# A Mamba-2 block with LoRA experts: the gates of six groups moved out of the scan into a stage of their own

## The chip, the cores and the metric

The kernel runs on one core of a Trainium2 chip, in one launch. The metric is the device time in microseconds (us). Engines: TensorE (PE in the profile; PEld is its weight load), VectorE (DVE), ScalarE (ACT), GpSimd (POOL) and SyncE (SP), whose queue issues all DMAs here. All data are fp32; a matmul of this kernel shows as two records of TensorE.

## What is computed

The input is x, 2048 tokens of 1024 channels. It is normalised (layer norm), goes through a Mamba-2 layer and a LoRA mixture, and both are added to x. The parts that matter here:

```python
proj = einsum('bld,pd->blp', xn, in_proj_w)      # gate 4096 | hbc 6144 | dt 64
gate, hbc, dt = proj[..., :4096], proj[..., 4096:10240], proj[..., -64:]
xBC = silu(causal_conv4(hbc))                    # x: 64 heads of 64; B, C: 8 groups of 128
state = state * dA_t + dtx_t * B_t               # the scan, over 2048 steps
y = state @ C_t + x * D
yn = y * rsqrt(mean(y * y over a group of 512) + eps) * norm_weight
yn = yn * silu(gate)
out = yn @ out_proj_w.T
result = x + out + (xn @ W_base.T + b_base) + lora
```

Each of the eight groups has 512 of the 4096 gate channels: four tiles of 128.

## The kernel before

**Tiling.** Channels lie on partitions, in tiles of 128. The tokens are cut into two halves of 1024 (s = 0, 1), each half into two of 512, each of these into four chunks of 128. A block is one (half, group, 512 tokens): 32 blocks of four chunks, 128 chunks.

**Products of one level.** Each input projection is done in pairs of output tiles, [2 tiles x 1024 channels] by [1024 channels x 1024 tokens], as a 2 x 2 block product with seven products in place of eight (Strassen's scheme in Winograd's form). `pair` (L450) makes the seven products, each of four matmuls with 512 columns, and adds them up in PSUM and in two temporary tiles. Their right operands, seven sums of blocks of xn, stay in SBUF for a half (`ops_of`); the left ones are weight blocks and four sums of them, made by GpSimd in `left_operands` (L413; the sums are L427) in the first half, stored, and loaded again in the second. Seven products leave four quarters. Per pair, ScalarE copies one product (L474), VectorE makes two temporaries (L478, L482) and three of the quarters (L531), ScalarE the fourth quarter (L529). `stored` (L523) then writes each quarter to DRAM; for a gate it passes through a SiLU on ScalarE first: L533, on what VectorE wrote in L531.

**The stream of pairs.** `in_pairs` (L557) yields the pairs: for each half and group, three for x, B and C and two for the gate; at last eight for the base weights, the second half before the first. 88 pairs, 616 products. `products(n, side)` takes n products from the stream and interleaves small steps of other work (side).

**The scan.** The main loop (L978) runs the chunks. One chunk: a product; the norm's mean if a block begins; `scan_b` (L731: the products ps_y, ps_e, ps_st with the chunk's operands, then ecp, y and the state on VectorE, the state's decay on GpSimd); the decay scan es of the next chunk on VectorE (L688, from dab, which a DMA brings); a product; `scan_a`'s ps_cb and its masked product with es (L702, dab); further products; transposes ps_xt, from which ScalarE makes xdt (L713) and xdd (L721). The convolution of the next block (L646 on VectorE, with SiLU L653 on ScalarE), the norm's squares (L797, L802) and the norm with the gate (L819, L822, L830) run as side steps; `norm_gate` multiplies by the gate (loaded by `load_gate`) and stores y. `plan` (L968) sets how many products have been taken by each chunk: 35 before the first, 315 after 60 chunks, 602 after 128. So a chunk takes four or five. From block 15 on, `out_sums` (L864) makes the block sums of the output weights on GpSimd (L83, tiles wo), one sixteenth per block; blocks 2 to 13 of the first half also carry the layer norm of the second half's tokens, in pieces that begin at blocks 2, 5, 8 and 11.

**The output stage.** Behind the scan the last 14 products of the stream run, then the output projection: four passes (half, half of the channels), each a product of [8 tiles x 2048 channels] by [2048 channels x 1024 tokens] in two levels: seven units of seven products, a product being eight matmuls with 256 columns. Order of the passes: second half of the tokens first.

**The order of the work.** Matmuls and transposes (`mm`, `transpose`) keep their program order; so do the SiLU of the convolution, xdt and xdd. Other instructions may be moved by the scheduler that builds the program.

```python
def products(n, side):
    ...
    for i in range(n):
        next(stream)
...
            products(1, parts[0])
            ...
            scan_b(*blk, c)
            ...
            products(1, parts[1])
            next(a, None)
            products(1, parts[2])
            products(1, parts[3])
            next(a, None)
```

Of the kernel before, what the change touches and what calls it, by code (L numbers as in the profile page):

```python
# [13 lines left out]
L = 2048  # L14
# [20 lines left out]
KH = KT // 2  # L35
NW = 12
PRE = 5
POST = 2
# [4 lines left out]
def mamba_lora_kernel(  # L43
# [19 lines left out]
    dram = ctx.enter_context(tc.tile_pool(name="dram", bufs=1, space=bass.MemoryType.DRAM))  # L63
    const = ctx.enter_context(tc.tile_pool(name="const", bufs=1))
    in_ctx = ExitStack()
    op = in_ctx.enter_context(tc.tile_pool(name="op", bufs=1, side="right"))
    wp = in_ctx.enter_context(tc.tile_pool(name="wp", bufs=NW, side="right"))
# [489 lines left out]
    def in_pairs():  # L557
        for s in range(NS):
            ops = lambda s=s: ops_of["x", s]
            for g in range(G):  # L560
                if s and g == 0:
                    load_ops(s)
                for q, (i0, i1) in enumerate(((0, 1), (2, 3), (4, 5))):
                    tis = [4 * g + i if i < 4 else 32 + 8 * (i - 4) + g for i in (i0, i1)]
                    key, name = f"x{g}_{q}", f"x_{s}_{g}_{q}"
                    quarters = halves(*(w_in[32 + t] for t in tis))
                    to = stored(raw_d[g], i0, s, AF.Copy)
                    if s + g + q:
                        yield pair(key, name, quarters, ops, to, s == 0)
                    else:  # L570
                        yield plain_pair(key, name, quarters, to)
                for q in range(2):
                    t = 4 * g + 2 * q
                    yield pair(
                        f"g{g}_{q}", f"g_{s}_{g}_{q}", halves(w_in[t], w_in[t + 1]), ops,
                        stored(gate_d[g], 2 * q, s, AF.Silu), s == 0,
                    )
# [8 lines left out]

    N_IN = NS * (5 * G + 4)
    stream = ahead(in_pairs())
# [195 lines left out]

    def load_gate(s, g, half):
        sg = p1.tile([P, 4, TB], F32, tag="sg", name=f"sg_{s}_{g}_{half}")
        at = s * TS + half * TB
# [28 lines left out]
    def norm_gate(s, g, half):  # L816
# [11 lines left out]
        for j in (0, 2):  # L828
            two = xg[:, j : j + 2, :]
            nc.vector.tensor_tensor(two, two, sg_of[s, g, half][:, j : j + 2, :], ALU.mult)  # L830
            nc.sync.dma_start(y_d[g][:, j : j + 2, at : at + TB], two)
            yield
# [17 lines left out]
    def base_sums(pool, i):  # L850
# [7 lines left out]
        for j, what in ((3, "s1"), (4, "s2"), (5, "s3"), (6, "s4")):  # L858
            d = dram.tile([P, KH, P], F32, tag=f"{what}_b{i}", name=f"{what}_b{i}_d")
            nc.sync.dma_start(d, t[:, j])  # L860
            kept[f"b{i}", what] = d
        yield

# [103 lines left out]

    plan = [(0, 7 * PRE), (n_slots // 2 - NQ, 7 * (5 * G + 5)), (n_slots, total)]  # L968

# [8 lines left out]
    for b, blk in enumerate(blocks):  # L978
# [16 lines left out]
        for c in range(NQ):  # L995
# [28 lines left out]
            a = scan_a(*follow) if follow else iter(())  # L1024
            parts = [side[i * len(side) // n : (i + 1) * len(side) // n] for i in range(n)]

# [3 lines left out]
            scan_b(*blk, c)  # L1030
            if b == 14 and c:
                next(left_sums)
# [15 lines left out]
            products(1, parts[2])  # L1048
            products(1, parts[3])
            next(a, None)  # L1050
# [4 lines left out]
            if b == 14:  # L1055
                left_sums = base_sums(wo, c)
                next(left_sums)
            if 0 <= b - 15 < 16 and c == 0:
# [13 lines left out]
            if (after, c) in ((1, 1), (2, 0)):  # L1072
                next(rest)
    norm_mean(*blocks[-1])
    for _ in norm_gate(*blocks[-1]):
# [6 lines left out]

    oa = ctx.enter_context(tc.tile_pool(name="oa", bufs=1, reuse_waits="tile"))
    ow = ctx.enter_context(tc.tile_pool(name="ow", bufs=7, reuse_waits="tile"))
    ot = ctx.enter_context(tc.tile_pool(name="ot", bufs=5, reuse_waits="tile"))
    passes = [(s, p) for s in (1, 0) for p in range(2)]
    units = (1, 2, 5, 7, 6, 3, 4)
    inner = (1, 6, 5, 2, 7, 3, 4)
    HT = TB // 2

# [21 lines left out]
    quarter_of = {}  # L1112
    place_pool = [oa] * 2

    def load_quarter(t, k, n):
# [6 lines left out]
        for h in range(2):  # L1122
            x = place_pool[place].tile(
                [P, KH, TB], F32, tag=f"q{place}_{h}", name=f"q_{t}_{k}{n}_{h}"
            )
            nc.sync.dma_start(x, y_d[4 * p + 2 * k + h][:, :, at : at + TB])
            parts.append(x)
# [36 lines left out]

    load_hw(1)
    for _ in range(7 * POST - 5):
        next(stream)
    next_ops = {}
    for _ in level_two(quarter_of[0, 0, 0], "0_0", next_ops):
        pass  # L1170
    for _ in stream:
        pass
    in_ctx.close()
    ob = ctx.enter_context(tc.tile_pool(name="ob", bufs=1, side="right", reuse_waits="tile"))
# [55 lines left out]
    load_quarter(0, 0, 1)  # L1230
    load_acc(1, 0, 0)

    kept_sum = None
    for t, (s, p) in enumerate(passes):
        last = t + 1 == len(passes)
        for u, i in enumerate(units):
# [16 lines left out]
            if t == 0 and u < 2:  # L1253
                if u == 0:
                    at(3, load_quarter, 0, 1, 1)
                    at(5, load_acc, 1, 0, 1)
                else:
                    at(1, load_acc, 1, 1, 1)
                    at(4, load_acc, 1, 1, 0)
            for u0, n, quarter in ((2, 0, (0, 0)), (4, 2, (1, 0)), (6, 1, (0, 1)), (6, 2, (1, 1))):  # L1260
# [10 lines left out]
            if p == 1:  # L1271
# [3 lines left out]
                if not last:  # L1275
                    for u0, n, quarter in ((2, 4, (0, 0)), (6, 3, (1, 1)), (6, 5, (0, 1))):
                        if u == u0:
                            at(n, load_acc, s - 1, *quarter)
            elif t and u == 0:
# [123 lines left out]
```

## Time and profile before

| | |
|---|---|
| median of 3 runs | 3451.87 us (3450.51 to 3454.31) |
| the profiled execution | 3453.59 us; its span 3451.8 us |
| TensorE | 3409.2 us busy, clock granted 0.997 |
| VectorE | 2501.2 us busy |
| ScalarE | 1164.7 us busy |
| GpSimd | 696.1 us busy |
| DMA | 769.83 MB, mean 223 GB/s |
| first ps_y of the scan, last ps_y | at 184.4 us, at 2678.5 us |

How to read it: the times of single instructions come from the profiled execution. A group of instructions is named by line, engine, operation and the tiles written and read; behind it stand its count, the busy time and the mean length, and what ended the idle time before it. A table by stretches gives each engine's busy time in a piece of the span. In the waits a line reads: who waited, for whom, us in total, times, longest. A busy TensorE is one that has a matmul in it.

### The profile page before, as it was taken

What the parts mean: (1) busy time and instruction counts of PE and PEld (TensorE: products, weight loads), DVE (VectorE), ACT (ScalarE), POOL (GpSimd) and SP (SyncE); (2) the same over time, 40 slices, a digit from 0 to 9 for tenths busy, and PEclk for the clock granted to TensorE, in tenths of its full rate; (3) what the DMA queues carried; (4) which work ended last, traced back from release to release, by engine and by line L of the source; (5) the groups of instructions that cost most, each with busy time, mean ns of one, the idle gap of its engine ahead of it and who ended that gap; (6) DMA issues with size and microseconds to landing.
All of it is one profiled execution on the core that took longest, in us unless ns stands there. A gap on an engine that the chain in (4) does not pass through costs nothing.

```text
span 3451.8 us, 38274 instructions
## 1 busy us (share of the span) xinstructions
PE 3409.2 (99%) x12818; PEld 1992.3 (58%) x12818; DVE 2501.2 (72%) x2861; ACT 1164.7 (34%) x3182; POOL 696.1 (20%) x443
## 2 busy tenths in 40 slices
PE   9999999999999999999999999999999999999999
PEld 7444544544545544454455445444444588888888
DVE  7548877877977877777787877777775466566665
ACT  2234453444444443444445444444442100000000
POOL 3122223222222211322223232222321000000000
PEclk9999999999999999999999999999999999999999
DMA  6546655655666676887778887777778687586654
GB/s 235 186 166 197 205 191 186 211 187 197 203 200 204 205 254 219 291 256 231 236 242 260 236 258 244 245 237 236 228 239 267 243 277 242 196 299 188 214 164 146
DMA packets 530324, 769.83 MB, mean 223 GB/s; under 512 B 35152, under 2 KB 264656, under 8 KB 527440
## 3 DMA queue, kind: packets, MB, share of 16 engines
q1 hardware_dynamic: 530128, 767.39, 68.7%
q8 instruction: 102, 1.67, 0.2%
q14 instruction: 94, 0.77, 0.1%
HBM read 516.64 MB, written 250.61 MB: 222 GB/s over the span
## 4 chain that ended last, share of the span: by engine, by line
PE 84%; DVE 9%; issue 3%; ACT 2%; DMA 1%; POOL 0%; SPq 0%; DVEq 0%; ACTq 0%; POOLq 0%
PE ps_x_x L79 12%; PE ps_x_w L79 8%; PE ps_a_x L79 8%; PE ps_y_x L79 8%; PE ps_x_g L79 7%; PE ps_a_w L79 6%; PE ps_y_w L79 6%; PE ps_y_g L79 5%; PE ps_a_g L79 4%; PE ps_y L79 3%; PE ps_e L79 3%; PE ps_st L79 2%; PE ps_x_b L79 2%; DVE xg L646 2%; PE ps_a_b L79 2%
## 5 line engine op out<-in xcount | busy, mean ns | idle before, releaser
L83 POOL TENSOR_TENSOR state<-state,tot 128x512 f32<-128x512 f32 x112 | 153.7, 1373 | 1326.0 <-PE ps_e L79 1199.8
L688 DVE TENSOR_TENSOR_SCAN es<-dab,here 128x1024 f32<-128x1024 f32 x128 | 304.6, 2380 | 83.4 <-ACT xdd L721 81.8
L646 DVE SCALAR_TENSOR_TENSOR xg<-rawx,cw,xg 128x512 f32<-128x512 f32 x384 | 339.2, 933 | 18.7 <-ACT xg L640 18.0
L79 PE MATMUL ps_x_w<-t,w 128*128 128x256 f32 x1344 | 303.8, 379 | 0.0
L713 ACT ACTIVATE xdt<-ps_xt,dt 128x64 f32<-128x64 f32 x1024 | 223.8, 333 | 209.7 <-PE ps_xt L88 209.7
L79 PEld LDWEIGHTS ps_x_w<-t,w 128*128 128x128 f32 x1344 | 255.4, 190 | 41.5 <-issue 7.7
L721 ACT ACTIVATE xdd<-xdt,es 128x64 f32<-128x64 f32 x1024 | 261.9, 388 | 0.0
L1340 ACT COPY s<-ps_a_w 128x512 f32<-128x512 f32 x28 | 16.4, 586 | 636.0 <-PE ps_a_w L79 555.5
L83 POOL TENSOR_TENSOR wo<-wo 128x512 f32<-128x512 f32 (+1 forms) x112 | 213.4, 1906 | 6.8
L79 PE MATMUL ps_a_w<-q,w 128*128 128x256 f32 x896 | 202.5, 379 | 0.0
L702 DVE TENSOR_TENSOR dab<-es,cbm 128x1024 f32<-128x1024 f32 x128 | 180.1, 1407 | 29.6 <-ACT cbm L698 29.6
L79 PEld LDWEIGHTS ps_a_w<-q,w 128*128 128x128 f32 x896 | 170.2, 190 | 23.6 <-issue 0.5
L79 PEld LDWEIGHTS ps_y<-dab,xdt 128*64 128x64 f32 x2048 | 114.6, 139 | 105.1 <-ACT xdd L721 38.7
L79 PE MATMUL ps_x_x<-op_again,s_x 128*128 128x512 f32 x384 | 172.7, 592 | 0.0
L79 PE MATMUL ps_y_x<-op_again,s_x 128*128 128x512 f32 x384 | 172.7, 592 | 0.0
L79 PE MATMUL ps_a_x<-op_again,a_x 128*128 128x512 f32 x384 | 172.7, 592 | 0.0
L79 PE MATMUL ps_x_x<-op,s_x 128*128 128x512 f32 x368 | 165.5, 592 | 0.0
L79 PE MATMUL ps_y_x<-op,s_x 128*128 128x512 f32 x368 | 165.5, 592 | 0.0
L79 PE MATMUL ps_a_x<-op,a_x 128*128 128x512 f32 x368 | 165.4, 592 | 0.0
L79 PE MATMUL ps_y<-dab,xdt 128*64 128x128 f32 x2048 | 146.6, 284 | 7.8 <-ACT xdt L713 7.8
L531 DVE TENSOR_TENSOR ev<-ps_x_x,s_x 128x512 f32<-128x512 f32 x94 | 64.5, 687 | 120.5 <-PE ps_x_x L79 116.1
L646 DVE SCALAR_TENSOR_TENSOR bc<-rawb,cw,bc 128x512 f32<-128x512 f32 x192 | 145.7, 790 | 1.9 <-ACT bc L640 1.0
(236 smaller groups left out, 6118.6 us busy)
## 6 DMA issues: line engine op xcount, KB each, us to landing
w<-w SPq DMA_DIRECT2D x196, 512.0 KB, 3.7
dab<-da_d SPq DMA_DIRECT2D x128, 512.0 KB, 5.5
raw<-ev SPq DMA_DIRECT2D x192, 256.0 KB, 3.3
a_x<-in_w_in_dram SPq DMA_DIRECT2D x168, 256.0 KB, 4.2
w<-wo SPq DMA_DIRECT2D x96, 448.0 KB, 4.3
ecp<-run_d SPq DMA_DIRECT2D x256, 128.0 KB, 4.0
gate<-ev SPq DMA_DIRECT2D x128, 256.0 KB, 3.9
sg<-gate SPq DMA_DIRECT2D x32, 1024.0 KB, 7.8
```

Source lines behind the costliest of these rows:

```text
L79: tc.keep_in_program_order(nc.tensor.matmul(*args, **kw))
L83: ins = nc.gpsimd.tensor_tensor(*args)
L531: nc.vector.tensor_tensor(e, ps, add, alu)
L646: nc.vector.scalar_tensor_tensor(dst[:, i, :], raw[:, i, k : k + TB], cw[:, ti, k : k + 1], dst[:, i, :], ALU.mult, ALU.add,)
L688: nc.vector.tensor_tensor_scan(es.rearrange("p h t -> p (h t)"), dab.rearrange("p h t -> p (h t)"), here, 0.0, ALU.mult, ALU.add,)
L702: nc.vector.tensor_tensor(ms, es, cbm.unsqueeze(1).to_broadcast([P, HG, Q]), ALU.mult)
L713: ins = nc.scalar.activation(xdt[:, h, :], x_t[:, h, :], AF.Copy, scale=dt_of[s][:, half * NQ + c, at : at + 1],)
L721: ins = nc.scalar.activation(xdd[:, h, :], xdt[:, h, :], AF.Copy, scale=es[:, h, Q - 1 : Q])
L1340: nc.scalar.copy(s1, pa)
```

## The change

Six of the eight groups (g < 6; an oct is two groups, eight tiles, and there are `NO = 3` octs) no longer have gate pairs in the stream. It has 64 pairs, 448 products; the plan's marks are 35, 224 after 60 chunks, 434 after 128, so a chunk takes three or four, and a fourth is only taken when the plan asks for it. In these groups `norm_gate` stores the norm without a gate, and no gate is loaded there.

Behind the stream a new stage makes the gates: for each half and each oct a product of [8 tiles x 1024 channels] by [1024 channels x 1024 tokens] in two levels: seven units (outer products) of seven inner products, each inner product four matmuls with 256 columns. The outer left sums are made on GpSimd (`oct_sums`): the first oct's in the last block of the scan, the others' in the new stage; `left_two` makes the inner ones on GpSimd for each unit. The inner right sums are made on VectorE (`right_two`) and kept for the half's three octs; the seven outer right sums of the second half are loaded again (`load_again`). Finished quarters are passed through a SiLU, multiplied by the stored norm, which is loaded for it, and stored to yg_d (`gated`). The output stage reads yg_d for these groups and takes the first half of the tokens first.

```diff
+NO = 3
...
-                for q in range(2):
+                for q in range(2 if g >= 2 * NO else 0):
...
-    N_IN = NS * (5 * G + 4)
+    N_S = 5 * G - 4 * NO
+    N_IN = NS * (N_S + 4)
...
     def load_gate(s, g, half):
+        if g < 2 * NO:
+            return
...
-            nc.vector.tensor_tensor(two, two, sg_of[s, g, half][:, j : j + 2, :], ALU.mult)
+            if g >= 2 * NO:
+                nc.vector.tensor_tensor(two, two, sg_of[s, g, half][:, j : j + 2, :], ALU.mult)
             nc.sync.dma_start(y_d[g][:, j : j + 2, at : at + TB], two)
...
+    def oct_sums(pool, tag, o, i):
...
+        for j, src in enumerate(halves(w_in[at], w_in[at + 2])):
+            nc.sync.dma_start(t[:, j], src)
+        yield
+        a11, a12, a21, a22 = (t[:, j] for j in range(4))
+        add(a22, a21, a22, ALU.add)
+        add(a21, a11, a21, ALU.subtract)
+        add(a11, a22, a11, ALU.subtract)
+        add(a12, a12, a11, ALU.subtract)
+        for j, src in ((5, a22), (7, a21), (6, a11), (3, a12)):
+            nc.sync.dma_start(s_d[o][j][:, q, m], src)
...
-    plan = [(0, 7 * PRE), (n_slots // 2 - NQ, 7 * (5 * G + 5)), (n_slots, total)]
+    plan = [(0, 7 * PRE), (n_slots // 2 - NQ, 7 * (N_S + 4)), (n_slots, total)]
...
-            products(1, parts[3])
+            products(min(n - 3, 1), parts[3])
...
+    order = (1, 2, 6, 5, 7, 3, 4)
+    gate_units = [(s, o, i) for s in range(NS) for o in range(NO) for i in order]
...
+    def left_two(u):
...
+        add(s1, a21, a22, ALU.add)
+        yield
+        add(s2, s1, a11, ALU.subtract)
+        yield
+        add(s4, a12, s2, ALU.subtract)
+        yield
+        add(a21, a11, a21, ALU.subtract)
+        yield
...
+    def gated(s, o, a, n, z):
...
+        for q in range(2):
+            nc.sync.dma_start(y[:, q], y_d[2 * o + q][:, 2 * a : 2 * a + 2, at])
+        yield
+        for q in range(2):
+            nc.scalar.activation(z[:, q], z[:, q], AF.Silu)
+            yield
+        for q in range(2):
+            nc.vector.tensor_tensor(z[:, q], z[:, q], y[:, q], ALU.mult)
+            nc.sync.dma_start(yg_d[2 * o + q][:, 2 * a : 2 * a + 2, at], z[:, q])
+            yield
...
+        if i == 2:
+            nxt[0].append(lambda a=c11, b=k_: big_add(a, b))
...
+        def put(m, n, ps, add):
+            dst = out[:, :, m, n * HT : (n + 1) * HT]
+            if i in (1, 2, 5, 7):
+                if add is None:
+                    nc.scalar.copy(dst, ps)
+                else:
+                    nc.vector.tensor_tensor(dst, ps, add, ALU.add)
+            else:
+                for part in (ps, add):
+                    if part is not None:
+                        nc.vector.tensor_tensor(dst, dst, part, ALU.add)
+
+        left, right = left_of.pop(u), right_of[s, i]
+        for n, j in enumerate(inner):
+            ps = {1: pa, 2: pa, 6: px, 7: px, 4: px, 5: py, 3: py}[j]
+            for q in range(2):
+                for k in range(KQ):
+                    mm(
+                        ps[:, q, :], left[j][:, q, k, :], right[j][:, k, :],
+                        start=(n < 3 and q + k == 0), stop=(k == KQ - 1), skip_group_check=True,
+                    )
...
+            for step in side[n]:
+                step()
...
-    passes = [(s, p) for s in (1, 0) for p in range(2)]
+    passes = [(s, p) for s in range(NS) for p in range(2)]
...
-            nc.sync.dma_start(x, y_d[4 * p + 2 * k + h][:, :, at : at + TB])
+            g = 4 * p + 2 * k + h
+            nc.sync.dma_start(x, (yg_d if g < 2 * NO else y_d)[g][:, :, at : at + TB])
```

## The prediction

> **What bounds the kernel now.** I read four views: the page, a table by stretches, the waits, and the timeline of a spot where TensorE stands still. The page first:
>
> ```profile
> span 3451.8 us, 38274 instructions
> ...
> PE 3409.2 (99%) x12818; PEld 1992.3 (58%) x12818; DVE 2501.2 (72%) x2861; ACT 1164.7 (34%) x3182; POOL 696.1 (20%) x443
> ...
> PE   9999999999999999999999999999999999999999
> PEld 7444544544545544454455445444444588888888
> DVE  7548877877977877777787877777775466566665
> ```
>
> TensorE is busy everywhere, and it has two stages: a scan stage (slices 3 to 31; VectorE at 7 to 8 tenths) and an output stage (VectorE at 6). The table by stretches puts numbers on both (columns: stretch, length, then busy time of PE, PEld, DVE, ACT, POOL, clock, DMA share, GB/s):
>
> ```profile
> 400.00:1400.00 1000.00, 988.23 (x3528) 504.54 (x3527) 779.30 (x994) 453.75 (x1213) 235.67 (x155) 1.00 0.64 208
> 1400.00:2600.00 1200.00, 1183.31 (x4291) 594.17 (x4290) 935.78 (x1003) 522.36 (x1482) 338.27 (x191) 1.00 0.78 244
> ```
> ```profile
> 1094.50:1182.70 88.20, 88.20 (x327) 47.25 (x326) 75.03 (x98) 38.92 (x106) 21.82 (x15) 1.00 0.63 206
> 2551.00:2625.30 74.30, 74.30 (x273) 37.34 (x272) 58.92 (x59) 30.56 (x90) 21.31 (x12) 1.00 0.74 237
> 3000.00:3200.00 200.00, 200.00 (x912) 173.05 (x911) 126.11 (x137) 5.27 (x9) 0.00 (x0) 1.00 0.72 240
> ```
>
> VectorE has 78% in the scan stage and TensorE loses only 11.8 + 16.7 = 28.5 us of 2200. The single stretches are one block (four chunks) each: block 11, which also carries a layer norm, block 30, and the output stage. Block 11 has VectorE at 85% and no idle TensorE, so a full VectorE alone doesn't stop it. Where TensorE does stand still, the waits and a timeline (VectorE, then ScalarE) tell why:
>
> ```profile
> ACT ev L533 <- DVE ev L531: 175.7, 63, 7.6
> ```
> ```profile
> 2304.70 5.43 DVE L797 SCALAR_TENSOR_TENSOR xg<-xg,dsk,y 128x512 f32<-128x512 f32 x4
> ...
> 2317.49 0.68 DVE L531 TENSOR_TENSOR ev<-ps_y_g,s_g 128x512 f32<-128x512 f32 x1
> ```
> ```profile
> 2318.20 0.63 ACT L533 ACTIVATE ev<-ev 128x512 f32<-128x512 f32 x1 [3.22 <-DVE ev L531]
> 2318.74 1.73 ACT L713 ACTIVATE xdt<-ps_xt,dt 128x64 f32<-128x64 f32 x8
> ```
>
> VectorE runs late (four L797 take 5.43 us where the median of one is 0.745 us), so the SiLU of a gate's eviction waits 3.22 us at the head of ScalarE's queue, and xdt (L713), on which TensorE's next scan products wait, stands behind it. TensorE loses 2.6 us there. Only gate pairs have that SiLU.
>
> **The change part by part.** *Removed from the scan:* 2 halves x 6 groups x 2 = 24 gate pairs of 7 products of 4 matmuls. One product takes 3.43 us (timeline of TensorE: one starts at 1899.68, what follows it at 1903.11): 168 x 3.43 = 576 us of TensorE. *Added behind it:* 2 x 3 x 7 = 42 units of 28 matmuls with 256 columns. The output stage runs just this shape: 912 records in 200 us, two a matmul, 0.2193 us a record, 56 records a unit: 12.28 us, 516 us in all. TensorE's own work falls by 60 us: seven eighths of the products are left, each at 2% more per column.
>
> *VectorE in the scan.* A gate pair's five adds (L478, L482, L531: 0.68 us) go, 0.49 us a product; so do two gate multiplies (L830, 1.217 us) in three blocks of four. Products per block fall from 18.7 to 12.6 in the first half (189 in 60 chunks by the new plan) and from 16.9 to 12.35 in the second (210 in 68). Block 30 (17 products): TensorE 74.3 - 4.65 x 3.43 = 58.3; VectorE 58.9 - 2.3 - 2.4 = 54.2 us, 93%. Block 11 (19): TensorE 88.2 - 22.0 = 66.2; VectorE 75.0 - 3.1 - 2.4 = 69.5: VectorE is over. GpSimd's sums for fresh weights (L427, 1.4 to 2.1 us, four a pair) fall by 0.9 pair in a first-half block, some 5 us less to collide with, worth 0 to 5 us of VectorE; I take 2. Over the four layer-norm blocks (85 to 87% now) the excess is 8 to 18 us; I take 12.
>
> *A rule against it.* The Trainium skill (Perfetto Trace Analysis, Optimization Strategy) says that where the most-contended engine changes from stage to stage, interleaving the stages may help. This change takes interleaving away: TensorE work that filled a VectorE-heavy stage gets a stage of its own. By the rule all that VectorE can't follow is lost; by the rows VectorE's total stays below TensorE's but in the layer-norm blocks, so the 12 us are all that throughput costs. The rest is a question of waits.
>
> *Waits in the scan* (28.5 us now). Some 15 us end behind the gate's SiLU; with a quarter of these pairs left, -11. The other 17 come of evictions and xdt that reach VectorE late. Its spare share goes from 22% to 7%, and waits for a queue grow about as the inverse: 17 to 52, +35. From both sides: +0 if they stay (blocks 8 and 11 have none at 85%), +88 if they grow sixfold. I take 35, since the trace's fullest blocks lie nearer to none.
>
> *Chunks lose one product of cover.* es starts as soon as xdd (L721) is done, its product with cbm (L702) is done 4 us or more before TensorE needs it; one product less leaves about 1 us: counted in the 35.
>
> *The new stage.* Per unit VectorE has five or nine adds of 0.69 us, with the gating and operand sums 51 us (68 in a half's first oct) of an oct's 86: covered. A product here is 1.75 us, and one accumulator (product 7, then 4) must be read within that: one add of 0.69 us fits, a 1.22 us multiply ahead of it doesn't. 0 to 1 us a unit; nearest row, the output stage, loses nothing with 3.5 us: 0.15 x 42 = 6 us. ScalarE's SiLU: 8 of 1.06 us an oct, covered. GpSimd: 4 sums a unit (L427 1.4 us, 5.6) and 4 more in 8 units: 11.2 of 12.28 us, covered, barely. DMA: weights 7 MB, gate in and out 8 MB, block sums 8 MB: 23 MB in 86 us, 267 GB/s; the page has slices of 299 with TensorE full. SP issues some 50 more in an oct, 0.4 us each, behind no wait but a store's, with units loaded two ahead. In the scan SP loses gate stores and loads. The last oct's gating lies beside output products; the new order of the halves costs nothing, since the last gates are read only in the fourth pass; the hand-over between stages waits for tiles freed five units earlier: 0 to 5 us, taken at 0 for that reason. The sums of the first oct in the last block use GpSimd at 1.6 us of 17 busy: 0.
>
> *The sum.* -60 - 11 + 35 + 12 + 6 = -18 us. The profiled execution took 3453.6 us (span 3451.8), the median of the runs is 3451.9; from that median 3434 us.
>
> **The rivals.** *No new waits:* blocks 8 and 11 as the model for all; waits keep their 17 us: 3451.9 - 60 - 11 + 12 = 3393; without the layer-norm excess 3381. For it: zero idle at 85%. Against: VectorE's spare falls to a third.
>
> *VectorE falls behind GpSimd (slower).* The output weights' sums take 20 us of GpSimd in each block of the second half, the weight sums much the same in the first. The skill (SBUF — State Buffer, Who interferes with whom) calls the shared port an exclusive lock: an operation with two SBUF inputs blocks while GpSimd reads. The four L797 lost 2.45 us to 4.5 us of such sums, about half, not all; by the rule a block would lose up to 20 us, by that row about 10, and the 54.2 us have this in them already. But the chunks that follow had 9 us of idle VectorE to catch up in; now it is about 1 us a chunk, so the lag of chunk 3 lasts into the convolution of chunk 1. Price: 3.5 us in each of 30 blocks, 105 in place of the 52: 3487. It decides from 60 + 11 - 12 - 6 = 53 us of added waits, 1.8 us a block.
>
> *Half of that* (2 us a block): 3451.9 within 0.2%, no change.
>
> *The short evictions:* 1 us lost in each unit and in each oct's catching up: +45, 3479. Against: VectorE is at 60 to 79% there.
>
> *It doesn't do what it says:* the diff drops 672 matmuls of 512 columns and issues 1176 of 256; no reading of it leaves the counts as they were. Excluded.
>
> **How the numbers follow.** Likeliest 3434 (0.45, own range 3410 to 3444); no new waits 3390 (0.12); half the lag 3452 (0.12); full lag 3487 (0.24); short evictions 3479 (0.07). A measurement tells about 0.2%, 7 us, from no change: faster 0.57, same 0.12, slower 0.31. The range 3388 to 3492 leaves out about 1 in 10 on either side.
>
> **What would show it.** Right: blocks of the second half of 59 to 61 us with 12 or 13 products, VectorE at 90 to 93%, the L533 wait down to a quarter, 42 units of 12.3 to 12.5 us. Wrong: blocks over 62 us with TensorE waiting on xdt or L531 (lag), ScalarE held by L802 or L653 in the SiLU's place, units over 13 us (evictions, GpSimd), or a gap before the output stage.

## The result, and the profile after

The changed kernel takes 3549.13 us (median of 4 runs, 3547.47 to 3550.23), beside 3453.09 us for the kernel before on the same chip: ratio 1.0278, 95% interval 1.0261 to 1.0296. It is slower by 96 us; the forecast was 18 us faster, and the time lies outside the range.

The page of the kernel after, its first lines and the rows of TensorE and VectorE:

```profile
span 3546.5 us, 40663 instructions
...
PE 3386.6 (95%) x13826; PEld 2202.4 (62%) x13826; DVE 2733.4 (77%) x3103; ACT 1187.5 (33%) x3179; POOL 973.4 (27%) x611
...
PE   9999998998999899999989999999999999999999
...
DVE  7568888888889798889889888666766676666665
```

TensorE was 9 in every slice before; now there are slices of 8, all of them in the scan, where VectorE has 8 and 9. The span grew by 94.7 us, so the time is lost inside the program. The table by stretches places it. First the kernel before (first half of the scan, second half, output stage), then the kernel after (the same, with the new stage as third line). The first number behind a stretch is its length, the second TensorE's busy time, the fourth VectorE's; the granted clock is third from the end:

```profile
184.40:1496.50 1312.10, 1299.98 (x4635) 659.95 (x4634) 1005.59 (x1237) 582.73 (x1589) 329.53 (x214) 1.00 0.64 209
1496.50:2678.50 1182.00, 1165.66 (x4238) 585.83 (x4239) 903.92 (x966) 507.12 (x1462) 313.59 (x176) 1.00 0.78 243
...
2742.40:3451.80 709.40, 704.48 (x3201) 607.81 (x3199) 446.40 (x472) 18.75 (x32) 0.00 (x0) 1.00 0.65 218
```
```profile
184.10:1252.90 1068.80, 996.02 (x3875) 526.85 (x3874) 906.47 (x1140) 549.88 (x1526) 257.84 (x166) 0.97 0.63 203
1252.90:2236.70 983.80, 932.59 (x3664) 481.48 (x3663) 865.60 (x894) 479.79 (x1413) 351.20 (x183) 0.99 0.82 252
...
2297.10:2833.90 536.80, 515.84 (x2354) 447.39 (x2352) 347.16 (x382) 86.53 (x115) 284.47 (x192) 0.99 0.64 218
2833.90:3546.50 712.60, 706.63 (x3200) 608.85 (x3200) 453.25 (x478) 19.20 (x33) 0.00 (x0) 1.00 0.67 227
```

Length less busy time is TensorE's idle time. In the scan it rises from 12.1 + 16.3 = 28.4 us to 72.8 + 51.2 = 124.0 us; the new stage adds 21.0, the output stage 1.1. Over the whole span it goes from 42.6 to 159.9 us: **+117**. TensorE's busy time in the scan should have fallen by the 576 us of the removed products, from 2465.6 to 1889.6; it is 1928.6, **39 us more than its work**. The new stage is busy for 515.84 us, the 516 of the forecast. So the span's +95 is -60 (less work) + 117 (idle) + 37 to 39 (the same work at a lower clock; 37 over the whole span: 3409.2 - 60 = 3349 would have been TensorE's busy time, it is 3386.6).

**Whom TensorE waits for.** The waits of TensorE, before and then after:

```profile
PE ps_nv L79 <- ACT xdt L713: 10.5, 4, 3.3
PE ps_y L79 <- ACT xdt L713: 7.8, 5, 4.6
```
```profile
PE ps_y L81 <- ACT xdt L716: 40.1, 11, 9.6
PE ps_xt L90 <- ACT bt L703: 34.4, 19, 7.5
PE ps_var L81 <- DVE lsq L266: 9.2, 3, 6.1
```

Both large ones name ScalarE, which is busy for a third of the time. They are queue waits, so the question is what stands ahead of bt and xdt. (In the new file the lines are shifted: xdt is L716, bt L703, the skip product L802, its square L807, the SiLU of a stored gate L535 behind L533, the convolution's bias L643, the small projections' exponential L332.) The waits of ScalarE after:

```profile
ACT y L807 <- DVE xg L802: 136.1, 47, 8.3
ACT xg L643 <- DMA y<-xg: 82.3, 23, 8.1
...
ACT ev L535 <- DVE ev L533: 32.6, 11, 11.0
```

The gate's SiLU, 175.7 us before, is down to 32.6. But two others stand at the head of the queue: the squares (109.9 us before, so hardly longer) and the bias of the next convolution, which waits until the stored norm has left the buffer that it writes (29.5 us before). One place of the first kind, ScalarE and then TensorE (start, length, engine, line; the bracket is idle time and who ended it):

```profile
1299.67 1.56 ACT L643 ACTIVATE bc<-rawb,cb,cw 128x512 f32<-128x512 f32 x2
1307.61 1.06 ACT L807 ACTIVATE y<-xg 128x1024 f32<-128x1024 f32 x1 [6.38 <-DVE xg L802]
...
1309.90 0.25 ACT L703 COPY bt<-ps_cb 128x128 f32<-128x128 f32 x1
```
```profile
1304.01 0.27 PE L90 MATMUL ps_cb<-ident,bc 128*128 128x128 f32 x1
1304.12 3.60 PE L81 MATMUL ps_y_x<-op_again,s_x 128*128 128x512 f32 x8
1310.20 0.66 PE L90 MATMUL ps_xt<-ident,xg 128*128 128x128 f32 x4 [2.48 <-ACT bt L703]
1310.69 5.30 PE L81 MATMUL ps_a_x<-op_again,a_x 128*128 128x512 f32 x8
```

The square waits 6.38 us for VectorE's skip product; the copy bt, whose operand ps_cb has been there since 1304.3, is stuck behind it; and TensorE, which may not start ps_xt before bt has freed the buffer, has just one product (3.4 us) to do meanwhile. In the kernel before two products lie there in all chunks but the first. ScalarE's wait has hardly changed in length; what lies beside it has. (Whether that explains the loss is tested in runs 6 and 7.)

One place of the second kind, ScalarE, VectorE, TensorE, and the table by stretches right behind it:

```profile
591.82 2.22 ACT L643 ACTIVATE xg<-rawx,cb,cw 128x512 f32<-128x512 f32 x3 [8.10 <-DMA y<-xg]
594.06 1.28 ACT L332 ACT_TABLE_LOAD   x1
595.36 0.31 ACT L332 ACTIVATE ex<-at 128x128 f32<-128x128 f32 x1
595.57 1.74 ACT L716 ACTIVATE xdt<-ps_xt,dt 128x64 f32<-128x64 f32 x8
```
```profile
595.02 0.28 DVE L331 TENSOR_TENSOR at<-dt,na 128x128 f32<-128x128 f32 x1
```
```profile
582.67 3.60 PE L81 MATMUL ps_x_x<-op,s_x 128*128 128x512 f32 x8
595.92 2.17 PE L81 MATMUL ps_y<-dab,xdt 128*64 128x128 f32 x16 [9.65 <-ACT xdt L716]
```
```profile
595.92:601.51 5.59, 5.59 (x26) 4.32 (x27) 5.59 (x10) 4.06 (x17) 1.26 (x1) 0.51 0.30 94
601.51:605.28 3.77, 3.77 (x13) 1.85 (x11) 3.77 (x5) 0.00 (x0) 0.12 (x1) 1.00 0.00 0
```

VectorE is full throughout (13.25 of the 13.25 us from 582.67 on). The norm it finishes late is stored late, the bias waits 8.10 us, the exponential stands next, and xdt behind both: TensorE loses 9.65 us. What ends last in front of xdt is the exponential, not the bias: its operand `at`, the end of a chain of small VectorE operations, is there only at 595.30, so that an earlier bias would not have let xdt start earlier. (Run 5 takes this exponential out of the way.)

Then the wait is paid a second time: for the next 5.6 us the granted clock is 0.51, and the sixteen ps_y matmuls take 2.17 us (1.09 at 613.12, at full clock). The stretches at half clock in the trace add up to 20.5 us before and 105.8 after (without the one that begins as the program ends). The Trainium skill (TensorE: Matmul & The Clock Gate, HAM oscillation) names idle gaps of more than about 3.4 us as what halves the clock. In this trace shorter waits are enough: of the 21 stretches eleven follow a wait of 3.5 us or more, ten only waits of 2.0 to 3.2 us (three others of that length leave the clock as it is), such as the 2.48 us at ps_xt above, behind which a product takes 5.30 us in place of 3.60. The same page (Terms) prices the loss at the half of the time at half clock, which makes an estimate of (105.8 - 20.5) / 2 = 43 us. Measured are 37 to 39: part of that time falls on waits that still run. Counted in the traces, TensorE is busy in 80.9 us of it (19.3 before), which accounts for 31 us; where the other 6 to 8 come from isn't shown.

**Which blocks lose.** The table by stretches for blocks 4, 9 and 10 of the kernel after, all with three products in most chunks; block 9 also carries the second part of a piece of the layer norm:

```profile
443.19:502.99 59.80, 59.80 (x233) 30.54 (x233) 54.57 (x62) 31.23 (x93) 15.99 (x11) 1.00 0.59 196
784.86:859.70 74.84, 64.39 (x244) 33.81 (x243) 61.66 (x103) 41.45 (x103) 18.20 (x12) 0.93 0.54 173
859.70:916.06 56.36, 56.36 (x225) 28.94 (x225) 48.80 (x55) 32.83 (x97) 13.93 (x10) 1.00 0.59 197
```

Blocks 4 and 10 have VectorE at 91 and 87% and lose nothing. In the first half 57.0 of the 72.8 us of idle time lie in the eight blocks that carry the layer norm, 14.1 in block 15, and under 2 in the seven others. So a chunk of three products doesn't wait as such; in this half it waits where more than the usual work comes through it. In the second half the idle time is spread, 0 to 9 us a block.

### The profile page after: what moved, and what is told of

The parts are those of the page before. It is cut to its first block, busy times and chain, and to the rows that moved or that the text cites. A ratio compares the mean times of both kernels' runs of the same rounds, so it can differ in the third digit from the quotient of the medians.

```text
span 3546.5 us, 40663 instructions
## 1 busy us (share of the span) xinstructions
PE 3386.6 (95%) x13826; PEld 2202.4 (62%) x13826; DVE 2733.4 (77%) x3103; ACT 1187.5 (33%) x3179; POOL 973.4 (27%) x611
## 3 DMA queue, kind: packets, MB, share of 16 engines
q1 hardware_dynamic: 535360, 796.75, 68.9%
## 4 chain that ended last, share of the span: by engine, by line
PE 60%; DVE 18%; DMA 8%; issue 6%; POOL 4%; ACT 3%; SPq 1%; DVEq 0%; POOLq 0%; ACTq 0%
PE ps_x_w L81 8%; PE ps_x_x L81 7%; PE ps_y_w L81 5%; PE ps_a_w L81 5%; PE ps_y_x L81 5%; PE ps_a_x L81 4%; PE ps_x_z L81 4%; DVE xg L649 3%; PE ps_y_z L81 2%; PE ps_a_z L81 2%; PE ps_y L81 2%; PE ps_e L81 2%; DVE xg L802 2%; PE ps_st L81 2%; DVE es L691 2%
## 5 line engine op out<-in xcount | busy, mean ns | idle before, releaser
L85 POOL TENSOR_TENSOR state<-state,tot 128x512 f32<-128x512 f32 x112 | 171.9, 1535 | 1015.8 <-PE ps_e L81 915.7
L691 DVE TENSOR_TENSOR_SCAN es<-dab,here 128x1024 f32<-128x1024 f32 x128 | 319.3, 2495 | 79.9 <-ACT xdd L724 56.1
L649 DVE SCALAR_TENSOR_TENSOR xg<-rawx,cw,xg 128x512 f32<-128x512 f32 x384 | 348.4, 955 | 28.5 <-ACT xg L643 27.5
L716 ACT ACTIVATE xdt<-ps_xt,dt 128x64 f32<-128x64 f32 x1024 | 223.8, 330 | 153.7 <-PE ps_xt L90 153.3
L85 POOL TENSOR_TENSOR wo<-wo 128x512 f32<-128x512 f32 (+1 forms) x112 | 234.2, 2091 | 11.9 <-DMA raw<-ev 5.1
L81 PEld LDWEIGHTS ps_y<-dab,xdt 128*64 128x64 f32 x2048 | 119.6, 140 | 144.4 <-ACT xdd L724 54.2
L705 DVE TENSOR_TENSOR dab<-es,cbm 128x1024 f32<-128x1024 f32 x128 | 167.0, 1305 | 19.4 <-ACT cbm L701 19.4
L429 POOL TENSOR_TENSOR s_x<-a_x,a_x 128x512 f32<-128x512 f32 x48 | 69.5, 1447 | 361.8 <-PE ps_x_x L81 111.6
L649 DVE SCALAR_TENSOR_TENSOR bc<-rawb,cw,bc 128x512 f32<-128x512 f32 x192 | 156.0, 837 | 0.7
```

The costliest lines, as they stand in the source:

```text
L81: tc.keep_in_program_order(nc.tensor.matmul(*args, **kw))
L85: ins = nc.gpsimd.tensor_tensor(*args)
L429: nc.gpsimd.tensor_tensor(t[what], t[x], t[y], alu)
L649: nc.vector.scalar_tensor_tensor(dst[:, i, :], raw[:, i, k : k + TB], cw[:, ti, k : k + 1], dst[:, i, :], ALU.mult, ALU.add,)
L691: nc.vector.tensor_tensor_scan(es.rearrange("p h t -> p (h t)"), dab.rearrange("p h t -> p (h t)"), here, 0.0, ALU.mult, ALU.add,)
L705: nc.vector.tensor_tensor(ms, es, cbm.unsqueeze(1).to_broadcast([P, HG, Q]), ALU.mult)
```

## The experiments

The expectations name the theories by letters. **A**: the short chunk. A chunk with three products leaves too little matmul work (cover) beside the chain VectorE - ScalarE - TensorE, so what stands at the head of ScalarE's queue is no longer hidden; order and cover decide. **B**: VectorE's work. It falls behind as such, and the place where it shows is of no account. **C**: GpSimd's sums, which slow VectorE (the slower rival of the prediction). Each edit is to the changed kernel unless it says otherwise.

**1. How much is moved.** `NO` sets how many octs' gates are moved out.

```diff
-NO = 3
+NO = 1
```


> Two groups' gates moved (one oct); a chunk takes 3.9 to 4.1 products. TensorE's own work falls by 20 us against before. Theory A: hardly a chunk has three products, so hardly an added wait: 3453 - 20 + 8 (the new stage's own waits) = 3441, with idle of TensorE near 50. Theory B: the same within 10 us. If the new stage itself were what costs, it would show here: over 3453.

```diff
-NO = 3
+NO = 2
```


> Four groups' gates moved (two octs) in place of six; a chunk then takes 3.6 products. TensorE's own work falls by 40 us against before. Theory A (cover: the added waits come in chunks with only three products, because ScalarE's queue then has no spare time before bt and xdt are due): some 40% of the chunks have three products, so some 40% of the 117 us of added idle and 37 us of half clock: 3453 - 40 + 60 = 3473. Theory B (VectorE's load as a whole): its spare share goes back to 16%, waits fall more than in proportion, +25: 3438.

One oct: 3468.68 us, ratio 1.0045 (1.003 to 1.006). Two: 3482.18, 1.0086 (1.0069 to 1.0102). With three (+96) the steps are +16, +13, +67. Both theories put one oct at about 3441 and missed. The new stage isn't the reason: outside the scan the idle time goes from 14.2 to 24.3 us, in the first half of the scan from 12.1 to 33.0. Worked out from the traces in the way of the tables above, for the two halves of the scan (p: products per chunk; share: VectorE's busy share):

| kernel | half 1: p, share, idle us | half 2: p, share, idle us | at half clock, us |
|---|---|---|---|
| before | 4.67, 77%, 12.1 | 4.2, 76%, 16.3 | 20.5 |
| one oct | 4.08, 80%, 33.0 | 3.9, 80%, 9.2 | 47.8 |
| two octs | 3.6, 83%, 53.2 | 3.5, 84%, 11.3 | 58.0 |
| three octs | 3.15, 85%, 72.8 | 3.09, 88%, 51.2 | 105.8 |

In the first half each oct costs some 20 us of idle time. The second half gains at first (fewer SiLUs of gates may be why; no run shows it) and has a knee behind 3.5 products. The two halves have two causes, or one cause with two thresholds; cover and load change together here, so the next runs part them.

**2. Less work for VectorE.** The convolution with two of its three taps on VectorE; the output weights' block sums on GpSimd left out.

```diff
-                for k in range(1, KW):
+                for k in range(1, KW - 1):
```


> The changed kernel with the convolution's last tap left out (six of its 18 operations on VectorE in a block, 4.6 to 6 us of 56). Theory B (load): the spare share of VectorE goes from 13 to 21%, idle of TensorE in the scan from 124 to some 45 us, the half clock from 37 to 10: 3549 - 105 = 3444. Theory A (order: squares, exponentials and bt on ScalarE's queue): only the waits that begin at the convolution go, about 25 with their half clock: 3524.

```diff
-        add(x, t[:, :, 0], t[:, :, 2], ALU.subtract)
-        store(6, x)
...
+            nc.sync.dma_start(to[:, 0:4], t[:, 0:4, m])
+            nc.sync.dma_start(to[:, 4:7], t[:, 0:3, m])
```


> The changed kernel with GpSimd's sums of the output weights left out (blocks are stored as loaded, the same bytes). Theory C (GpSimd holds VectorE up at the shared port): the added idle of the second half of the scan, some 58 us, goes with some 15 of half clock: 3478; the layer-norm blocks of the first half stay as they are. Theory A: the lag of VectorE shrinks by 5 us of 56 in a block, waits by a third: 3525.

3486.76 us (-62) and 3500.68 us (-48), a single run each: between A's figure and the other's in both cases. The sums are indeed paid by VectorE: without them its busy time in the second half is 770.3 in place of 865.6 us with the same 894 instructions, 6 us a block:

```profile
1245.32:2192.35 947.03, 924.92 (x3663) 477.68 (x3663) 770.27 (x894) 479.23 (x1414) 102.42 (x64) 0.99 0.84 264
```

In the first half, where those sums lie in the last block alone, the idle time stays (68.9); in the second it falls to 22.1, and with two taps to 24.4. Neither reaches the 9 to 11 of one or two octs.

**3. Both at once, and the opposite at another cover.** First the two edits of run 2 together, then two octs with one tap more:

> The changed kernel with both left out: the convolution's last tap and GpSimd's sums of the output weights. VectorE's share in the second half falls to some 76%, that of the kernel before, with three products a chunk as in the changed kernel. Theory B: idle in the second half falls from 51 to 16 or less, as before the change. Theory A: the waits of a short chunk stay, 22 as in each of the two edits alone. The first half as with the two taps alone, 56: 3475 by B, 3484 by A.

```diff
-NO = 3
+NO = 2
...
-                for k in range(1, KW):
+                for k in (1, 2, 3, 3):
```


> Four groups moved (3.6 products a chunk), and VectorE loaded more: the convolution's last tap is applied twice, six operations more in a block, 4.6 to 6 us. VectorE's share in the second half of the scan goes from 84% to some 90%, as in the changed kernel, with half a product more of cover. Theory B (VectorE's load): idle in the second half 11 to 40 or more, in the first 53 to 75, with half clock +25: 3482 + 75 = 3557. Theory A (cover: only three products in a chunk make waits): idle rises by 10 in all: 3495.

3485.18 us with both taken away, no better than with two taps alone, and 3532.29 us for two octs with a tap more (+50 over two octs). The second half of the scan in the table by stretches, of the one and then of the other:

```profile
1223.40:2173.86 950.46, 924.92 (x3663) 477.99 (x3663) 707.49 (x804) 478.91 (x1414) 95.77 (x64) 0.99 0.85 263
```
```profile
1361.05:2398.35 1037.30, 1013.10 (x3871) 515.89 (x3871) 934.17 (x1005) 490.09 (x1431) 361.05 (x183) 1.00 0.80 252
```

With 3.09 products a chunk and VectorE at 707.5 / 950.5 = 74%, less than in the kernel before, TensorE is still idle for 25.5 us; with 3.5 products and VectorE at 90% it is 24.2. The time of the first is A's (3484), that of the second lies between the two forecasts. So B alone fails (a load of 74% doesn't bring 3.09 products to the 11 us of 3.5 at 84%) and so does A alone: at 3.09 products the idle time goes from 24 to 51 us as the load goes from 83 to 88%, and at 3.5 from 11 to 24 as it goes from 84 to 90%.

**4. The load at the old cover.** The kernel before with one tap more (the second edit above, at its line 645):

> The kernel before with VectorE loaded more: the convolution's last tap applied twice (six operations more in a block), VectorE from 76% to 82% in the second half, with 4.2 products a chunk. Load alone: idle in the second half 16 to 25, as with 3.6 products at 90%; 3453 + 25 = 3478. Load only with a short chunk: idle stays under 20: 3458.

3483.52 us, 31 over the kernel before. Idle 25.2 and 21.7 us at 81 and 82%. A load that costs 3 us of idle time a per cent in the first half and 1 in the second, where the full change has 85 and 88% and costs 61 and 35: the load has a price at any cover, but it isn't the whole.

**5. Edits at the head of ScalarE's queue.** The squares one product later; the exponential one step later (A's local remedies).

```diff
-                parts[1] += steps(sq, 2)
-                parts[2] += steps(sq, 1)
+                parts[2] += steps(sq, 2)
+                parts[3] += steps(sq, 1)
```


> The changed kernel with the norm's squares one step later in the chunk, so that bt stands ahead of the second of them on ScalarE's queue. Theory A (what stands ahead of bt on ScalarE's queue decides): the 25 us of waits of ps_xt for bt go, with some 8 of half clock; idle in the second half of the scan 51 to 28: 3549 - 33 = 3516. Theory B (VectorE's load): the late VectorE only shows elsewhere, in xdt or the norm's mean: 3543 or more.

```diff
-        nc.scalar.activation(ex, at, AF.Exp)
         yield
+        nc.scalar.activation(ex, at, AF.Exp)
```


> The changed kernel with the exponential of the decay (ScalarE, behind a chain of some 20 VectorE operations) issued one step later, in the layer-norm blocks only. Theory A: the waits of ps_y for xdt behind it (13 us, and 5 to 8 more that follow from them) and their half clock go: 3549 - 25 = 3524, idle in the first half of the scan 73 to 55. Theory B: no change, 3549 within 5.

3557.23 us (+8) and 3529.60 us (-20). The first fails. The second takes the first half's idle time from 72.8 to 52.3 us and leaves the second about as it was (54.1): taking this one head of the queue away gives its price back. With the squares it doesn't.

**6. The copies off ScalarE.** If ScalarE's order is the cause, cbm and bt on VectorE's queue should free TensorE.

```diff
-        nc.scalar.copy(cbm, psm[:, 0, :])
+        nc.vector.tensor_copy(cbm, psm[:, 0, :])
...
-        nc.scalar.copy(bt, psm[:, 1, :])
+        nc.vector.tensor_copy(bt, psm[:, 1, :])
```


> The changed kernel with the copies cbm and bt made by VectorE in place of ScalarE (0.27 us each there): two operations more on VectorE in every chunk, some 2 us a block. If ScalarE's queue ahead of bt is what costs in a short chunk, the 34 us of waits of ps_xt go and the idle of the second half falls from 51 to 30: 3549 - 30 = 3519. If VectorE's own lateness is what costs, ps_xt waits for VectorE instead and idle rises to 55 to 65: 3560.

3556.33 us, and TensorE's first wait in this kernel is

```profile
PE ps_xt L90 <- DVE bt L703: 72.9, 49, 7.2
```

in place of 34.4 us behind ScalarE's bt; the second half's idle time is 53.4 us. The wait changed its carrier and grew: the copies now stand in the queue of VectorE, which is late itself. Taking them off ScalarE's queue doesn't help.

**7. A product put back at its place.** Counted in TensorE's trace, chunk by chunk: with one product between ps_cb and ps_xt TensorE waits at ps_xt in 18 of 113 chunks after, 34 us; with two in none of 14 after, and in none of 127 before. But with two octs 57 chunks have one product there, at a lower load of VectorE, and wait for 0.7 us in all. To see what the place is worth, a product was moved there from ahead of ps_cb.

```diff
-            products(1, parts[1])
+            if n > 3 or c == 0:
+                products(1, parts[1])
             next(a, None)
+            if n == 3 and c:
+                products(1, parts[1])
             products(1, parts[2])
```


> The changed kernel with one product put elsewhere: in a chunk of three products (the first chunk of a block aside) the second one is issued behind ps_cb and its transpose in place of ahead of them, so that two products again lie between ps_cb and the transposes ps_xt, as in every chunk of the kernel before; the work is the same. Counted in the trace of the changed kernel: with one product there, TensorE waits at ps_xt in 18 of 113 chunks, 34 us; with two, in none of 14; in the kernel before in none of 127. Theory A (cover at this place): the waits at ps_xt fall to under 12 us, the products ahead of ps_y are as many as before, so its 45 us stay; the time falls by 20 to 40 us with the clock, to 3510 to 3530. Rival B (VectorE's backlog sets the time, and the place of a product only says where the wait shows): the waits move to ps_y or the other products' operands, and the time stays within 8 us of 3549.

And with the exponential of run 5 besides:

> The same, and the exponential of the small projections one step later, which alone took 20 us off the changed kernel (3549 to 3530), by waits at ps_y. Theory A: the two are at different places and add up: 3490 to 3510. Rival B: no more than the exponential alone, 3522 to 3538.

3559.08 and 3540.01 us. The waits of TensorE in the first of them:

```profile
PE ps_nv L81 <- ACT xdd L724: 17.3, 7, 3.1
PE ps_nv L81 <- DVE y L810: 12.6, 8, 3.2
...
PE ps_xt L90 <- ACT bt L703: 8.5, 2, 8.0
```

The wait at ps_xt is all but gone, 34.4 to 8.5, and 24 us more have come at the sum of squares ps_nv (29.9; in the changed kernel 2.9 behind y and 2.7 behind xdt); idle time in the scan 130 us (124). At this place A is refuted (3510 to 3530), and B comes nearer (within 8 us of 3549; it is 10): the wait goes where VectorE's lateness is met next. Part of that is the edit's own making: the side steps that ride on the moved product move with it, in the last chunk of a block the squares that ps_nv waits for. So the run shows that this move doesn't help, not that no order would. The later exponential still gives its 19 us.

**8. The new stage.** The sums of the second and third oct left out on GpSimd:

```diff
-        add(a22, a21, a22, ALU.add)
...
+        if o == 0:
+            add(a22, a21, a22, ALU.add)
...
```


> The changed kernel with GpSimd's sums for the second and third oct left out (blocks are stored as loaded, the same DMAs), so that GpSimd has four operations a unit in the new stage throughout. If GpSimd's queue costs there: the 8 us of waits for its left sums and part of VectorE's lateness go, the stage takes 537 - 10 = 527: 3539. If it is VectorE's order alone: 535 or more, 3547.

3540.36 us (-9), which is by luck the figure forecast for GpSimd's queue (3539): the new stage was to fall to 527 us for it. The stage in the table by stretches

```profile
2291.40:2825.10 533.70, 514.86 (x2354) 447.73 (x2352) 340.95 (x382) 85.03 (x114) 229.74 (x160) 0.99 0.64 217
```

is 3 us shorter: 18.8 us idle in place of 21.0; TensorE's waits for GpSimd there (7.2 us) are gone, and its waits for VectorE have grown. Another 4 of the 9 us lie in the first half of the scan, which the edit doesn't touch: differences of that size between single runs say nothing. These sums are not what the stage loses.

**9. Can it be mended?** The plan with three products in most chunks and the spare ones in the eight blocks that carry pieces of the layer norm (2, 3, 5, 6, 8, 9, 11, 12), here with two octs:

```diff
-NO = 3
+NO = 2
...
+        if slot <= first:
+            spare = 7 * (N_S + 4) - 7 * PRE - 3 * first
...
+            return 7 * PRE + 3 * slot + spare * full // (NQ * len(norm_blocks))
```


> Four groups moved, and the products of the first 60 chunks laid where the layer norm is: three a chunk elsewhere, a bit over four in blocks 2, 3, 5, 6, 8, 9, 11 and 12. Theory A (cover in the chunk is what lacks): idle in the first half of the scan falls from 53 to 25, half clock by 8: 3482 - 36 = 3446. Theory B (load of VectorE in these blocks, which stays the same per block while TensorE has more to do there): the same, since more time passes per block: 3450; in the other blocks, with three products and no layer norm, idle stays under 10 by B, rises by 15 by A: then 3461.

With the two edits of run 5 besides:

> Four groups moved, with the products laid where the layer norm is, the exponential one step later and the squares behind bt. Theory A: idle in the first half of the scan 53 to 18, in the second unchanged at 11, half clock near that of the kernel before: 3482 - 45 = 3437, below both kernels. Theory B: 3450.

One oct (`NO = 1`), the plan and the exponential:

> Two groups moved, the products of the first 60 chunks laid into the layer-norm blocks (five a chunk there, three elsewhere), the exponential one step later. By both theories the layer-norm blocks are as full of products as before the change and idle in the first half falls from 33 to 12, half clock by 8 us: 3469 - 29 = 3440, below both kernels. If chunks with three products cost by themselves (A), 5 to 10 more.

And the later exponential alone, in the kernel before, with no gate moved:

> The kernel before with the exponential one step later. It loses some 5 us behind that exponential (waits of xdt and xdd), so 3447 to 3449 at best by A; no difference, 3451, by B.

Two octs with the plan: 3472.11 us (-10 to two octs); with all three edits 3454.16 (3446.25 to 3459.78; ratio 1.0007, 0.9998 to 1.0016). One oct with plan and exponential: 3446.40, ratio 0.9982 (0.9976 to 0.9989), at 27.3 us of half clock. The kernel before with the exponential alone: **3438.70 us, ratio 0.9957 (0.9945 to 0.997)**, faster than both kernels. Its first half in the table by stretches:

```profile
183.46:1480.65 1297.19, 1294.92 (x4633) 656.15 (x4632) 1005.15 (x1237) 582.62 (x1589) 334.35 (x214) 1.00 0.65 212
```

15 us shorter than the kernel before's, 2.3 us idle in place of 12.1. The first two lie above both theories' figures (with the plan alone the first half is still idle for 40.0 us, where A had 25), the third is A's, and the fourth gained three times what was forecast. So what made the mended versions competitive was not the moved gates: with them, the best is 7.7 us behind the version without (the two differ in the plan as well).

## Why the prediction was wrong

**TensorE's own work: right.** -60 us; the new stage's busy time is 515.84 us against 516 forecast, and a removed product 3.43 us.

**The gate's SiLU: right, and given back.** Its wait is down to 19%, where a quarter was forecast. (The 2.6 us that TensorE loses in its example are 2.45 in the trace.) But the 11 us credited for it came from work that was queued behind it waiting for the same late VectorE. With the SiLU gone the squares, the bias and the exponential stand at the head, and of these the prediction had the squares alone, as a sign ("ScalarE held by L802 or L653 in the SiLU's place"; L653 is the convolution's SiLU), with no price.

**VectorE's load: too low in the second half.** Block 30 was put at 54.2 us of VectorE. It has

```profile
2127.59:2192.19 64.60, 57.66 (x232) 29.71 (x231) 59.12 (x57) 28.22 (x86) 22.22 (x12) 1.00 0.82 283
```

59.1, and 58.9 before: nothing fell. One reason is a reading: block 30 multiplies block 29's norm, whose group keeps its gate, so the 2.4 us of gate multiplies don't go there. The other is that the operations left take longer: over the 15 full blocks of that half VectorE falls from 58.4 to 55.8 us, by 2.6, where some 4 were forecast. Those blocks last 62.6 us on average, beyond the 59 to 61 named as the sign of being right. VectorE's total still stays below TensorE's own work.

**The waits in the scan: the step that failed.** "17 to 52, +35" with +88 as the far end, and 12 for the layer-norm blocks; less the 11, that is +36. Measured: 28.4 to 124.0, **+96**. The choice of the near end rested on blocks 8 and 11, "none at 85%". Those had 19 products of cover. With 12 or 13 the eight blocks that carry the layer norm are idle for 3.8 to 12.9 us each, 57.0 us in all (11.8 before), where the prediction gave 12 us to four of them; block 11 alone, one of the two models, goes from 0 to 3.8, block 8 from 0 to 6.1. The 12 were put down to a VectorE that is over its time, but it is busy for 78 to 93% of these blocks: it is waits that cost there, behind the small projections' exponential above all (run 5: 20 us). The second half, for which the models were to speak too, adds 35. A stretch without waits at a high load shows that load harmless at its cover, and the change took the cover away and raised the load at once (runs 2 to 4). The Trainium skill's rule on interleaving, quoted in the prediction, spoke for this loss; the prediction let throughput decide against it.

**A chunk's lost product: the wrong place.** The prediction looked at es and dab, and found about 1 us left. The chains that came late were others: skip product, square, bt, and in the layer-norm blocks the small projections, exponential, xdt.

**The clock: not in the sum.** +37 us. Every wait was priced at its length. Waits, from some 2 us on, are mostly followed by work at half clock, so that the added 96 us in the scan cost 135.

**The new stage: mis-sized.** 21.0 us idle against 6; 12.78 us a unit (536.8 / 42), just over the 12.3 to 12.5 forecast. The waits are spread over GpSimd's left operands (7.2 us, 4 times, for ls) and several of VectorE's (k, c and s_z, some 2 to 3 us each); leaving out the oct sums took 2 of the 21. The rival of the short evictions had put 45 us more there: too many.

**The slower rival: right in direction.** VectorE's lag does carry over into the next chunks. It was put at 3487: idle time +95, no term for the clock. Measured were +117 and +37. Its mechanism, GpSimd's sums, is a real part (48 us with the clock, run 2), but less work on VectorE does as much, so C is one source of the load and not the cause. The row it was priced from is read too mildly: of the two sums' 4.57 us only 3.47 fall beside the four skip products, which lost 2.45 to them, seven tenths and not half.

**What stays open.** In the second half cover and load act together; the runs give the grid of points above, no law. A rival stands untested: in a chunk of three products the last quarter of the side steps is issued with no product beside it; a kernel that spreads them over the three wasn't run. Why the squares' chain can't be placed so that nothing is met isn't shown: two attempts to move it failed, and VectorE's order is set by the scheduler. A second buffer for what L643 writes wasn't tried.

## What to carry to other kernels

Filler that is taken out of a stage of long chains takes cover from them and loads the other engines more densely, and the two together cost more than each: in the second half here +9 us of idle time with the short cover at 74%, +5 with the old cover at 82%, +35 with the short cover at 88%. Shares of busy time alone don't price it: count for each step of the loop how much work of the bound engine lies beside its longest chain before and after, and take a full, waitless stretch as evidence only for the cover that it has. When a waiter is removed from the head of a queue, price the next one that waits for the same late engine. Price each wait of more than some 2 us with the slow clock behind it: here 40% on top.

## What the runs showed of the hardware

A wait of 9.65 us was followed by 5.59 us at a granted clock of 0.51, and waits of 2.0 to 3.2 us were followed by half clock ten times; in this kernel 105.8 us at half clock, though the mean clock of the execution is still 0.985. GpSimd's block sums (351.2 - 102.4 = 249 us in the second half) cost VectorE 95 us of busy time at the same instructions: 0.38 us for each of GpSimd's.
